# Two of four scaled token tiles take their places from another ring (L3 attention of a four-layer decoder)

## The chip, the core and the metric

The kernel is one program on one core of a Trainium2 chip. The core has five queues of instructions that run side by side: TensorE (PE, with its weight loads listed apart as PEld), VectorE (DVE), ScalarE (ACT), GpSimd (POOL) and SyncE (SP, which here only issues transfers). The metric is the device time of one execution in microseconds; lower is better. The time before is 3500.77 us, the median of three executions (3495.93 to 3503.63).

## The reference, cut to what matters

The reference runs four decoder layers over x of shape (8, 256, 256): 8 batches of 256 tokens with 256 features. Each layer is an attention, a cross attention and a feed-forward part, each added to x and normalised. The change lies in the attention of the last layer (L3), which is a state-space block rather than a softmax attention:

```
h = _rmsnorm(x, rms_w)
zxbcdt = h @ in_proj_w.T
...
conv = conv_b
for k in range(D_CONV):
    conv = conv + xp[:, k:k + l, :] * conv_w[:, k]
xBC = jax.nn.silu(conv)
...
dt = jax.nn.softplus(dt + dt_bias)
...
y = _ssd(xh, dt, A, B, C)
y = y + xh * Dp[None, None, :, None]
y = _rmsnorm(y * jax.nn.silu(z), norm_w)
out = y @ out_proj_w.T
return out + res
```

Only the first line concerns the change: every row of x is multiplied by its own 1/root-mean-square, and the scaled x must then lie transposed (features on partitions) for the product with in_proj_w. The weight rms_w is multiplied into in_proj_w elsewhere.

## The kernel before

**Tiles.** x lies in 16 tiles of 128 tokens x 256 features, X[0] to X[15]. Four tiles make a block of 512 tokens (blocks 0 to 3, called B0 to B3 below), and two tiles make a batch (batches 0 to 7). The L3 attention, `l3_attn`, works per block for what is cheap to do for 512 tokens at once, and per batch for the rest.

**A block.** `block(blk)` first waits for its X tiles (`need`), takes the reciprocal roots r of the mean squares on POOL (L183, L184, 128x4), and then, for t = 0 to 3, writes the scaled tile x = X * r (L2054 on ACT for block 0, L2056 on POOL for blocks 1 to 3), transposes it on PE (`transpose_to`, two instructions a tile at L302, eight a block), and copies the result from PSUM to the tile xr (`copy`, L142 on DVE and L144 on ACT in turn). `steps` then forms dt and its running sums for the block (L2071 to L2094).

**A batch.** `inputs` makes z, x, B and C (PE, L156), the convolution on DVE (L2148 and L2152) and two Silu passes on ACT. `weights` makes the decay matrices (PE L2176; DVE L2189 and ACT L2187; exp on ACT L2199; products on DVE L2206 and L2213). `outputs(b)`, called O0 to O7 below, makes y (PE L2227, DVE L2230, POOL L2235), its mean square (ACT L2239, PE L156, DVE L2245, POOL L183 and L184), and then, for each of the batch's two tiles: x2 = X + X on POOL (L2251), the output product on PE, r = product * r2 + x2 on DVE (L2255), and the layer norm of r (DVE L253, L255; POOL L183, L184; DVE L264), which is the new X tile.

**Rings.** The pool `tmp` keeps three places for each tag. A tile asked for under a tag takes one of its three places in turn, so it can be written only when the tile that held the place before has been read for the last time. Two tags matter here, both with places of 128x256 float32: "xb", which holds the four scaled tiles of a block and the x2 of `outputs`, and "res", which holds the r of `outputs` and, in the other layers, the r of `finish` (L280). Before the change, the xb places are asked for in this order: B0 t0 to t3, B1 t0 to t3, O0 x2 twice, B2 t0 to t3, O1 twice, O2 twice, B3 t0 to t3, O3 twice, and so on; the res places in the order O0 twice, O1 twice, O2 twice.

**Order.** The instructions are written in a Python program, with generators (`later`, `tick`, `fill`, `following`) that weave pieces of one batch between those of another. What is written is not yet the order of a queue: when the program is built, a planner goes through it with estimated durations, hands out the places of the rings, and fixes each engine's order; an instruction that is ready early by the plan can go ahead of one written earlier. In the trace, for one, x2 of batch 0 (L2251, 3013.12 us) runs ahead of the y product of the same batch (L2235, 3040.47 us), which is written before it. On the chip each engine then keeps its fixed order and waits at every instruction for what that needs.

Of the kernel before, what the change touches and what calls it, by code (L numbers as in the profile page):

```python
# [20 lines left out]
P = 128  # L21
NB = 8
S = 256
D = 256
# [37 lines left out]
class Build:  # L62
# [1916 lines left out]
    def l3_attn(self):  # L1979
        nc, a = self.nc, self.a  # L1980
        with ExitStack() as ctx:
# [62 lines left out]
            def block(blk):  # L2044

                self.need(2 * blk + 1)
                out = xrs[blk] = self.t(w2, [P, 2, 512], "xr")
                r = self.t(self.sm, [P, 4], "r4")
                self.rsqrt(r, self.ms[blk], 1.0, 1e-5)
                yield  # L2050
                for t in range(4):
                    x = self.t(self.tmp, [P, D], "xb")
                    if blk == 0:
                        nc.scalar.activation(x, self.X[4 * blk + t], AF.Copy, scale=r[:, t : t + 1])  # L2054
                    else:
                        nc.gpsimd.tensor_scalar(x, self.X[4 * blk + t], r[:, t : t + 1], 1.0, ALU.mult, ALU.mult)  # L2056
                    self.transpose_to(out[:, :, t * P : (t + 1) * P], x, 2)
                yield
                yield from steps(blk, out)

            def steps(blk, xr):
# [36 lines left out]
                sts[blk] = dt, cs, csT.rearrange("p i s -> p (i s)")  # L2098

            front = block(0)  # L2100
            fill(5)
            next(front)
# [167 lines left out]
            Es.append(self.t(w3, [P, 4, 384], "E", bufs=1))  # L2270
            xds = [free[:, 3072:].rearrange("p (t h d) -> p t h d", t=2, h=8), self.t(w3, [P, 2, 8, 64], "xd", bufs=1)]
            following = block(1)
            next(following)
            for b in range(NB):
                blk = b // 2
                if b % 2 == 0:
                    next(following, None)

                self.tick()
                E, xd = weights(b, cv, *sts[blk])  # L2280
                last = (b, cv, zs, E, xd)
                if b + 1 < NB:
                    cv, zs = inputs(b + 1, xrs[(b + 1) // 2])
                    if b % 2 == 0:
                        next(following, None)
                self.settle(1)
                if b % 2:
                    following = block(b // 2 + 2) if b // 2 + 2 < NBLK else iter(())
                    next(following, None)
                self.later(outputs(*last))  # L2290
# [672 lines left out]
```

## Time and profile before

| | |
|---|---|
| median of three executions | 3500.77 us (3495.93 to 3503.63) |
| the profiled execution | 3466.69 us, of which the span shown is 3465.0 us |
| TensorE clock granted, mean | 0.913 |
| the first scaled tile (L2054) | 2920.87 us after the span's start |
| the last scaled tile (L2056) | 3133.4 us |
| L2056 (POOL) | 12 times, 472 / 478 / 2693 ns (least, median, most) |
| L2054 (ACT) | 4 times, 493 / 502 / 510 ns |
| L2251 (POOL) | 16 times, 605 / 612 / 2055 ns |

The profile is of one execution, which was 34 us shorter than the median of the three timed ones. Times in it are counted from the start of its span. A row of the timeline gives start, duration, engine, line, operation, the tile written and the tiles read, shapes and count; in brackets stands how long the engine was idle before it and what ended that. Rows of a kind on one engine are merged, with a count. A row of the chain (the work that ended last, followed back) gives start, duration, engine, tile and line.

### The profile page before, as it was taken

The numbers are of one execution on the slowest core, as the hardware profiler recorded it, in microseconds if no ns is written. First come the engines' busy times: TensorE is split into PE (matmuls) and PEld (weight loads), VectorE is DVE, ScalarE is ACT, GpSimd is POOL, SyncE is SP. The second block draws the span as 40 slices with busy tenths as digits, with TensorE's granted clock in tenths as the row PEclk, the third lists the DMA queues.
The fourth block names the chain that finished last, engine by engine and source line by source line (L and its number), as shares of the span: only waits on it lengthen the run. The fifth ranks groups of instructions, "written<-read, shape, count | busy, mean of one in ns | idle before, by whom it ended". The sixth has DMA issues, their size and how long they took to land. (4 is left out here: it accounts for less than half of the span.)

```text
span 3465.0 us, 49405 instructions
## 1 busy us (share of the span) xinstructions
PE 3068.0 (89%) x19135; PEld 2169.0 (63%) x19146; DVE 1819.0 (52%) x4852; ACT 1055.4 (30%) x2386; POOL 911.1 (26%) x1370
## 2 busy tenths in 40 slices
PE   4777679989998998998999999898888998888789
PEld 3444357768886666665566776565555886676556
DVE  7887556641005656785111221576675344777652
ACT  4666422222222233332111111343222112344211
POOL 2222323343313211232000000322343454322241
PEclk6777779989999999999999999999777999988899
DMA  9900110025532000001010333100002562000000
GB/s 334 333 1 6 34 42 16 16 94 185 187 128 89 17 28 14 17 17 59 14 37 25 113 131 118 37 20 8 7 19 84 200 210 77 25 1 7 13 6 19
DMA packets 132672, 241.58 MB, mean 70 GB/s; under 512 B 14600, under 2 KB 103952, under 8 KB 124752
## 3 DMA queue, kind: packets, MB, share of 16 engines
q1 hardware_dynamic: 108176, 138.34, 11.8%
q0 software_dynamic: 23104, 98.95, 8.3%
q8 instruction: 155, 2.54, 0.3%
q10 hardware_dynamic: 1152, 1.05, 0.1%
q14 instruction: 85, 0.70, 0.1%
HBM read 158.61 MB, written 79.69 MB: 69 GB/s over the span
## 5 line engine op out<-in xcount | busy, mean ns | idle before, releaser
L156 PE MATMUL ps<-xt,w 128*128 128x256 f32 (+1 forms) x1408 | 444.6, 465 | 8.3 <-issue 8.3
L156 PE MATMUL ps<-w,hT 128*128 128x256 f32 (+1 forms) x1792 | 397.4, 380 | 0.0
L156 PEld LDWEIGHTS ps<-w,hT 128*128 128x128 f32 (+1 forms) x1792 | 330.5, 187 | 55.9 <-issue 6.0
L156 PE MATMUL ps<-gT,w 128*128 128x256 f32 (+1 forms) x1472 | 356.9, 401 | 5.7 <-ACT gT L144 3.0
L156 PEld LDWEIGHTS ps<-xt,w 128*128 128x128 f32 x1408 | 263.8, 194 | 150.5 <-issue 129.8
L156 PEld LDWEIGHTS ps<-gT,w 128*128 128x128 f32 x1472 | 276.8, 191 | 76.1 <-ACT gT L144 3.9
L156 PE MATMUL ps<-w,oT 128*128 128x256 f32 x768 | 184.1, 394 | 12.3 <-DVE oT L1423 11.2
L156 PEld LDWEIGHTS ps<-w,oT 128*128 128x128 f32 x768 | 147.7, 196 | 48.6 <-issue 12.6
L1147 ACT ACTIVATE hT<-ps,more 128x256 f32<-128x256 f32 x152 | 71.9, 473 | 199.1 <-PE ps L156 199.1
L236 PE MATMUL ps<-ident,x 128*128 128x128 f32 x320 | 64.8, 314 | 74.2 <-DVE x L264 57.3
L276 POOL TENSOR_TENSOR xb<-x,rows 128x256 f32<-128x256 f32 x96 | 74.0, 778 | 212.7 <-DVE res L281 205.5
L264 DVE TENSOR_SCALAR x<-res,mv,rs 128x256 f32<-128x256 f32 x128 | 58.8, 459 | 123.0 <-POOL rs L184 123.0
L1158 DVE COPY y<-ps 128x512 f32<-128x512 f32 x41 | 28.3, 690 | 174.6 <-PE ps L156 174.6
L1224 DVE TENSOR_TENSOR hT<-hT,ps 128x512 f32<-128x512 f32 x56 | 38.5, 687 | 150.6 <-PE ps L156 150.6
L686 ACT ACTIVATE e<-ps,nm 128x128 bf16<-128x128 f32 (+1 forms) x256 | 103.7, 459 | 40.1 <-DVE nm L681 24.1
L1220 ACT ACTIVATE hT<-ps 128x512 f32<-128x512 f32 x56 | 33.4, 597 | 238.5 <-PE ps L156 238.5
L1717 POOL TENSOR_TENSOR kpad<-kpad,rows 128x256 f32<-128x256 f32 (+1 forms) x10 | 7.3, 729 | 363.5 <-DVE hu L1666 276.2
L236 PEld LDWEIGHTS ps<-ident,x 128*128 128x128 f32 x320 | 39.5, 155 | 98.9 <-DVE x L264 44.9
L903 POOL TENSOR_TENSOR P<-P,z 128x1232 f32<-128x1232 f32 (+1 forms) x32 | 55.2, 1734 | 167.3 <-DVE z L902 167.3
L970 PE MATMUL ps<-PT,V 77*64 77x256 f32 x512 | 90.8, 413 | 6.9 <-ACT PT L144 4.4
L1581 ACT ACTIVATE f<-ps,neg 128x512 f32<-128x512 f32 x128 | 77.3, 688 | 57.7 <-PE ps L1578 57.7
L1582 DVE SCALAR_TENSOR_TENSOR f<-ps,f 128x512 f32<-128x512 f32 x128 | 79.1, 682 | 26.1 <-ACT f L1581 26.1
(665 smaller groups left out, 6344.7 us busy)
## 6 DMA issues: line engine op xcount, KB each, us to landing
l2x<-zero SPq DMA_DIRECT2D x28, 1024.0 KB, 11.4
l0x<-zero SPq DMA_DIRECT2D x16, 1024.0 KB, 11.4
w<-in_L_ffn_rg SPq DMA_DIRECT2D x8, 1024.0 KB, 7.1
w<-in_L_ffn_ru SPq DMA_DIRECT2D x8, 1024.0 KB, 5.0
w<-in_L_ffn_rd SPq DMA_DIRECT2D x8, 1024.0 KB, 5.4
l2e<-y SPq DMA_DIRECT2D x22, 256.0 KB, 2.3
rows<-in_rows SPq DMA_DIRECT2D x9, 544.0 KB, 3.7
l0e<-y SPq DMA_DIRECT2D x19, 256.0 KB, 2.7
```

The source lines that it names most:

```text
L156: self.nc.tensor.matmul(out, lhsT, rhs, start=(i == 0), stop=(i == last))
L236: self.nc.tensor.transpose(ps[:, k * P : (k + 1) * P], x[:, k * P : (k + 1) * P], self.ident)
L264: nc.vector.tensor_scalar(t, r, mv[:, 0:1], rs, ALU.subtract, ALU.mult)
L276: self.nc.gpsimd.tensor_tensor(t, self.X[i], row, ALU.add)
L686: nc.scalar.activation(e[:, : (t + 1) * P], ps[j][:, i, :], AF.Exp, bias=nm[:, t, h : h + 1], accum_out=z[:, t, h : h + 1],)
L903: eng.tensor_tensor(pr, pr, z.unsqueeze(2).to_broadcast([P, n, SC]), ALU.mult)
L970: nc.tensor.matmul(po[64 * m : 64 * m + 64, :S], V[:, h * 64 : (h + 1) * 64], ahead[n % 2][:, m, :], start=True, stop=True,)
L1147: nc.scalar.activation(hT[:, f + m, :], ps[:, m * 256 : (m + 1) * 256], func, bias=more[:, f + m : f + m + 1])
L1220: nc.scalar.activation(hT[:, f, :], ps, func, **({"bias": bias(f)} if bias else {}))
L1224: nc.vector.tensor_tensor(hT[:, f, :], hT[:, f, :], ps, ALU.mult)
L1581: nc.scalar.activation(f[:, j], ps[j], AF.Exp, bias=neg1)
L1582: self.mark = nc.vector.scalar_tensor_tensor(f[:, j], ps[j], 1.0, f[:, j], ALU.max, ALU.min)
```

## The change

The scaled tile is asked for under the tag "xb" for t = 0 and 1, as before, and under "res" for t = 2 and 3. Sizes, engines and arithmetic stay as they are, and so do the number of instructions and the memory taken. The order in which places are asked for becomes: on xb, B0 t0 t1, B1 t0 t1, O0 twice, B2 t0 t1, O1 twice, O2 twice, B3 t0 t1, O3 twice; on res, B0 t2 t3, B1 t2 t3, O0 twice, B2 t2 t3, O1 twice, O2 twice, B3 t2 t3, O3 twice.

```diff
                 for t in range(4):
-                    x = self.t(self.tmp, [P, D], "xb")
+                    x = self.t(self.tmp, [P, D], "xb" if t < 2 else "res")
                     if blk == 0:
                         nc.scalar.activation(x, self.X[4 * blk + t], AF.Copy, scale=r[:, t : t + 1])
```

## The prediction

> **What bounds the kernel now.** I read the page first, for the whole span.
>
> ```profile
> span 3465.0 us, 49405 instructions
> ...
> PE 3068.0 (89%) x19135; PEld 2169.0 (63%) x19146; DVE 1819.0 (52%) x4852; ACT 1055.4 (30%) x2386; POOL 911.1 (26%) x1370
> ```
>
> PE bounds the kernel as a whole, but the change sits in one late stage, so next come the stage's own windows: before, during and after the batches of L3 attention.
>
> ```profile
> 2870.00:3010.00 140.00, 118.53 (x461) 80.69 (x459) 76.63 (x238) 41.89 (x67) 61.79 (x102) 0.93 0.19 61
> 3010.00:3240.00 230.00, 194.21 (x1104) 160.38 (x1104) 174.59 (x444) 100.03 (x159) 53.00 (x83) 0.84 0.01 3
> 3240.00:3465.00 225.00, 184.45 (x744) 130.53 (x744) 90.92 (x264) 38.07 (x69) 62.12 (x116) 0.92 0.04 15
> ```
>
> (Columns: length, then busy PE, PEld, DVE, ACT, POOL, clock, DMA.) From 3010 to 3240 us PE is busy 84% and DVE 76%: they take turns, and neither is full. POOL, which writes 12 of the 16 scaled tiles, is busy 53 of 230 us. So a POOL wait costs only through who waits for POOL. The view of the writing line says that:
>
> ```profile
> L2056 POOL TENSOR_SCALAR xb<-x,r x12: 472/478/2693, 2943.3 to 3133.4; 128x256 f32<-128x256 f32 x12
> ...
>   DVE res L2255: 15.2, 3
>   DVE x L264: 9.5, 1
>   PE ps L302: 6.5, 2
> ...
>   PEld ps L302: 8.9, 3
>   PE ps L302: 8.3, 2
> ```
>
> The first three indented rows are what POOL waited for before writing: 15.2 us in 3 waits for the r of `outputs` (an xb place still held by an x2), 9.5 us once for a new X tile, 6.5 us in 2 waits for transposes (the place held by this block's own first tile). The last row is what it costs others: PE waited 8.3 us in 2 waits. Both are in the timeline:
>
> ```profile
> 3064.02 2.69 POOL L2056 TENSOR_SCALAR xb<-x,r 128x256 f32<-128x256 f32 x1 [4.79 <-PE ps L302]
> ...
> 3066.76 0.44 PE L302 MATMUL ps<-ident,xb 128*128 128x128 f32 x2 [2.42 <-POOL xb L2056]
> ...
> 3132.14 1.73 POOL L2056 TENSOR_SCALAR xb<-x,r 128x256 f32<-128x256 f32 x2 [9.45 <-DVE x L264]
> ...
> 3133.47 1.14 PE L302 MATMUL ps<-ident,xb 128*128 128x128 f32 x4 [5.88 <-POOL xb L2056]
> ```
>
> The first pair is the ring: B2's fourth tile waits for the transposes of its first, and PE then waits 2.42 us for it. The second pair is not: B3's third and fourth wait for X[14] and X[15] (DVE L264), which DVE wrote only at 3131.62 and 3132.34. Last I read the chain of what ended last, around the first pair:
>
> ```profile
> 3055.55 0.48 DVE res L2255
> 3056.04 0.66 DVE st L253 x2
> ...
> 3056.87 0.27 POOL rs L183
> ...
> 3058.40 0.20 POOL rs L183
> ...
> 3060.73 1.58 DVE w L2152 x4
> ...
> 3066.85 2.65 DVE w L2152 x4
> ...
> 3070.56 0.40 DVE w L2230
> ...
> 3071.01 1.52 PE ps L2227 x16
> ```
>
> The chain runs through DVE's convolution from 3059.3 to 3071, not through the late tile. PE's 2.42 us lie beside it: at 3071.01 PE waits again, for DVE L2230.
>
> **The change part by part.** It removes and adds no instruction; 16 scale instructions keep their 0.478 us (POOL) or 0.502 us (ACT), and no DMA and no SP work is touched. What moves is when a place is free, and with it the planned order.
>
> B0 (ACT, 2920.87 to 2931.45). Three tiles are written at 2920.87 to 2922.66, the fourth at 2930.94 behind B0's own transposes. With res free (its last earlier use, in routing, is at 2652 us) the fourth can follow the third. The chain there is ACT: two scaled tiles, hTs (L1907), the third tile, hTs, to 2923.15. If the fourth goes ahead of the last hTs, that is late by 0.50 us; if behind, ACT is idle 2.66 us soon after, and it costs nothing. PE's wait of 0.43 us at 2931.50 goes, but at that time the chain is in POOL's rsg and DVE's L264. I take 0, bounds -0.43 and +0.50.
>
> B1 (POOL). Three tiles run at 2943.33, the fourth at 3012.67. It now follows the third at about 2944.7, and O0's first x2 (0.61 us) can follow that; POOL is idle 7.44 us until 2952.17, and the gathers queue after it, so nothing is pushed. At 3012 the chain runs in PE without a gap: 5 transposes 1.17, 4 products 0.64, 3 transposes 0.74 us. Contiguous or not, they cost the same. I take 0; the bound below is -1.89 us, PE's wait just before (for POOL L2306, ended 3011.02), if the order let all transposes (1.17 + 0.74 = 1.91 us) fill it; above, 0.
>
> B2 (POOL). The first and second tile wait as before: t1 for O0's first r (3054.48). t2 no longer needs O0's second x2 place; t3 takes the place of O0's first r and waits for its norm (L264, 3057.80 + 0.41 = 3058.21) instead of B2's first transposes (3063.9). It is written some 5.5 us earlier. PE's 2.42 us go, covered by DVE, which is busy without a gap from 3059.3 to 3075; were that cover gone, up to -2.42. On the other side POOL's queue holds the two root pairs of O0's norm (3056.87 and 3058.40), which DVE's L264 waits for on the chain. O1's first x2 (0.61 us) becomes free at O0's second r (3056.03) and can slip in behind t2 (ends 3056.61): to 3057.22, that is 0.35 us past 3056.87. t3, ready at 3058.21, ends at 3058.69 against 3058.40: +0.29. Taken: +0.64. Bounds: -2.42 and +0.61 + 2.69 = +3.30 (the longest L2056 in the trace).
>
> One rule speaks here. The row: L2056 lasted 2.69 us at 3064.02, beside DVE's L2148 and L2152 back to back, against 0.478 in the median. The Trainium skill, "SBUF — State Buffer", section "Who interferes with whom", says that GpSimd and VectorE share one port pair, that an instruction which finds it held blocks until that one ends, and that a VectorE instruction with two SBUF inputs contends with a GpSimd one that reads. By that rule a moved tile waits for one L2152 (0.48), so t3 costs 0.96, and the sum of B2 would be about 0.35 + 0.77 = +1.1 us; by the row it is up to 2.5.
>
> B3 (POOL). t2 and t3 take places of O1 and O2 (r read by 3123.2), but X[14] and X[15] come at 3132 all the same. New waits on DVE: the r of O1 and O2 now need B2's transposes (about 3066) done; they are written at 3086.9 and 3118.5, so no wait. PE's 5.88 us stay: 0. Bounds: the nearest row is that wait itself, -5.88 if a new order puts O3's L2227, which stand behind it, first; +5.88 if such a wait arises once more.
>
> Later. O4 to O7 and the two parts after them ask for places as before. Their order can still change, since the planner's clock is shifted. Nearest row: PE's wait of 5.54 us for DVE L264 at 3244.51, so -5.54 to +5.54; taken 0.
>
> Sum: 0 + 0 + 0.64 + 0 + 0 = +0.6 us on the profiled 3466.69 us, 3467.3. On the median (34.08 us above the profiled execution) that is 3501.4; the terms know nothing below 1 us, and I say 3500. Ends: -0.43 - 1.89 - 2.42 - 5.88 - 5.54 = -16.2 and 0.50 + 3.30 + 5.88 + 5.54 = +15.2.
>
> **The rivals.**
>
> Same (the forecast): the orders stay nearly as they are, the removed waits were covered, and the tag of a place that wasn't what held B3 is no help. For it: the chain above. Time 3500, by itself 3494 to 3507.
>
> Faster: the earlier tiles let the planner order PE and DVE anew between 3010 and 3240. For it: PE and DVE are both idle at times there (36 and 55 us), and a fixed order that waits for one tile while 24 L2227 stand behind it (3133.47) is the kind of thing that a small shift undoes. Against: X[14] and X[15] don't depend on the rings changed. Price: 5.88 + 2.42 = 8.3 us, 3492.5; with B1's 1.89, 10.2 us, 3490.6. It decides against "same" from 7 us, that is, only if the 5.88 goes.
>
> Slower: the scaled tile and x2 that are free sooner go ahead of O0's root on POOL (+3.30 at most at B2), and the new order gives PE one more wait like that of 3133.47 at a place where the chain passes: +3.30 + 5.88 = 9.2 us, 3510. For it: four roots of two batches lie between these tiles, and POOL stretched L2056 to 2.69 us once. Against: it needs the second wait; the first alone is under 7 us. It decides when both fall on the chain.
>
> The change does nothing: if places are handed out in written order, B2's t3 waits as long as before by the plan, and all orders are equal. Time 3501, part of "same".
>
> **How the numbers follow.** 0.2% is 7 us, about what a measurement of this kernel tells from no change (the three runs span 7.7). "Same" gets 0.38, since no term that I take reaches 2 us. That the one planned order has to stand through 540 us is less sure than that: a shift of ready times reaches every queue from 2921 us on. So faster gets 0.36 and slower 0.26; faster is the larger, as every place is free no later than before, and only POOL's queue can lose. The range goes to both sums of ends, little widened for the runs' own spread: 3500.8 - 16.2 - 2 = 3482 and 3500.8 + 15.2 - 1 = 3515.
>
> **What would show it.** Right: L2056 has no wait for L302 any more; B1's four tiles stand in one row near 2943; PE's wait at B2's last transposes is gone; the chain between 3056 and 3071 still runs through L2152; the wait before B3's last transposes is still there, for L264. B2's step is wrong if POOL's roots of O0's norm come at the same time after the r as now. The prediction is wrong if the stretch from B2 to O7 gets shorter or longer by more than 7 us with other instructions in front of PE's waits, or if the difference lies after 3240 us, where nothing was changed.

## The result, and the profile after

The changed kernel takes 3499.55 us (median of 12 executions, 3491.84 to 3510.07) against 3499.94 us for the kernel before in the same comparison (12 executions, 3490.62 to 3506.93). The ratio is 1.0 with a 95% interval of 0.9987 to 1.0013: no difference that can be measured. The forecast was 3500.

The profiled execution after is 33.5 us longer than the one before, and that says nothing of the change. The page of after:

```profile
span 3498.5 us, 49398 instructions
...
PE 3086.9 (88%) x19135; PEld 2175.4 (62%) x19146; DVE 1817.6 (52%) x4852; ACT 1055.6 (30%) x2386; POOL 909.2 (26%) x1370
```

The 7 instructions fewer than before are semaphore instructions; the engines' counts are equal. The first scaled tile stands at 2953.32 us in it, against 2920.87: 32.45 of the 33.5 us are there before the first instruction that the change touches, where both programs have the same order of work. Nor does that part belong to the change: in a second profile of the changed kernel, shown below, the first scaled tile stands at 2924.48 us. So the change is read from the first scaled tile to the end: 544.10 us before, 545.17 after. The kernel before, profiled a second time, has 545.16, and the changed one 542.43.

The planned order hardly moved either. With the names of the places set aside, PE and SP issue the same sequence in both kernels (between 98 and 355 us, far ahead of the change, the records of some neighbouring matmuls stand in exchanged places). ACT has one instruction moved (B0's fourth tile, now ahead of the last hTs), DVE three (at about 2925 to 2937 us) and POOL eight.

What the change was to do, it did. The writing line in after, with what POOL waited for and who waited for it:

```profile
L2056 POOL TENSOR_SCALAR xb<-x,r x6: 472/479/482, 2977.0 to 3152.5; 128x256 f32<-128x256 f32 x6
L2056 POOL TENSOR_SCALAR res<-x,r x6: 472/477/1272, 2977.9 to 3167.5; 128x256 f32<-128x256 f32 x6
...
  DVE res L2255: 13.7, 2
  DVE x L264: 4.1, 1
...
  PE ps L302: 6.6, 1
```

The 6.5 us that POOL waited for transposes (L302) before a scaled tile are gone, and so is the tile of 2.69 us. PE's two waits for scaled tiles, 8.3 us, have become one of 6.6. The ring's wait itself has not gone from POOL, though: it is now the x2 of `outputs` that wait for transposes, 11.2 us in 3 waits, where before it was 0.5 us in one. No engine waits for an x2 in either kernel. The line of x2 in after:

```profile
L2251 POOL TENSOR_TENSOR xb<-x x16: 604/612/2055, 2978.8 to 3271.7; 128x256 f32<-128x256 f32 x16
...
  PE ps L302: 11.2, 3
```

POOL's timeline around B1 and B2 (start, duration, what it wrote, and in brackets the idle time before):

```profile
2976.97 0.94 POOL L2056 TENSOR_SCALAR xb<-x,r 128x256 f32<-128x256 f32 x2
2977.89 0.93 POOL L2056 TENSOR_SCALAR res<-x,r 128x256 f32<-128x256 f32 x2
...
3087.91 0.48 POOL L2056 TENSOR_SCALAR xb<-x,r 128x256 f32<-128x256 f32 x1 [6.01 <-DVE res L2255]
3089.56 0.61 POOL L2251 TENSOR_TENSOR xb<-x 128x256 f32<-128x256 f32 x1 [1.17 <-DVE res L2255]
...
3091.75 0.48 POOL L2056 TENSOR_SCALAR res<-x,r 128x256 f32<-128x256 f32 x1 [0.55 <-DVE mv L255]
...
3097.91 2.43 POOL L2251 TENSOR_TENSOR xb<-x 128x256 f32<-128x256 f32 x2 [4.76 <-PE ps L302]
```

B1's four tiles stand in one row. B2's fourth comes at 3091.75, 4.4 us after O0's first r (3087.33), where before it came 10.1 us after it (3064.02 against 3053.90). PE in the same stretch, and at B3:

```profile
3097.44 0.60 PE L302 MATMUL ps<-ident,xb 128*128 128x128 f32 x4
3097.88 0.60 PE L302 MATMUL ps<-ident,res 128*128 128x128 f32 x4
...
3104.43 0.87 PE L2227 MATMUL ps<-E,xd 128*64 128x256 f32 x8 [3.42 <-DVE w L2230]
...
3167.56 1.15 PE L302 MATMUL ps<-ident,res 128*128 128x128 f32 x4 [6.55 <-POOL res L2056]
```

The wait of 2.42 us at B2's last transposes is gone. The next one has grown in its place, from 1.28 us (3071.01, before) to 3.42, for the same DVE L2230: 3.70 us of waits became 3.42. At B3 PE waits for the same tile as before, 0.67 us longer (6.55 against 5.88 us). And the chain of work that ended last runs through DVE's convolution, as before:

```profile
3093.18 0.41 DVE x L264
...
3094.65 1.58 DVE w L2152 x4
...
3099.25 0.62 DVE w L2148
3099.87 1.15 DVE w L2152 x2
...
3101.34 1.58 DVE w L2152 x4
...
3103.98 0.40 DVE w L2230
...
3104.43 1.52 PE ps L2227 x16
```

Batch by batch, the two kernels lie on each other. The table gives the time from the first r (L2255) of one batch to that of the next, from the timelines, in us:

| | O0 | O1 | O2 | O3 | O4 | O5 | O6 | sum |
|---|---|---|---|---|---|---|---|---|
| before | 33.0 | 31.6 | 34.7 | 30.3 | 27.7 | 26.0 | 21.0 | 204.4 |
| before, second profile | 32.9 | 31.4 | 35.0 | 31.4 | 30.5 | 25.9 | 21.0 | 208.1 |
| after | 32.9 | 31.7 | 35.1 | 30.3 | 29.7 | 24.1 | 20.9 | 204.7 |
| after, second profile | 33.2 | 30.5 | 35.1 | 30.3 | 29.7 | 25.1 | 21.3 | 205.2 |

O4 differs by 2.8 us between two executions of the same kernel before. What differs there is the clock that TensorE was granted (0.94 in the first, 0.83 in the second). It is not steady in this stage: it switches between full and half speed. In before, after PE's wait of 2.42 + 1.28 us in O0 and one of 3.34 us in O1 (columns: stretch, length, busy PE, PEld, DVE, ACT, POOL, granted clock, DMA):

```profile
3076.00:3083.00 7.00, 7.00 (x26) 6.19 (x26) 1.91 (x4) 4.05 (x5) 0.91 (x2) 0.51 0.01 4
3083.00:3103.00 20.00, 15.51 (x105) 12.71 (x106) 19.28 (x59) 6.77 (x12) 2.72 (x7) 1.00 0.00 0
3103.00:3114.00 11.00, 10.83 (x51) 9.45 (x46) 4.98 (x13) 6.73 (x9) 3.40 (x4) 0.53 0.01 1
```

In after the same two drops come, as long as before and, within 0.2 us, at the same distance from the batch's r:

```profile
3109.70:3116.30 6.60, 6.60 (x23) 5.79 (x23) 1.84 (x4) 3.77 (x5) 0.91 (x2) 0.50 0.02 4
3116.50:3137.00 20.50, 16.07 (x111) 13.03 (x109) 19.78 (x60) 7.41 (x14) 2.72 (x7) 1.00 0.00 0
3137.00:3147.20 10.20, 9.92 (x42) 8.86 (x39) 4.34 (x12) 6.09 (x7) 3.40 (x4) 0.50 0.01 2
```

The last row reads: in 10.2 us at half speed, PE was busy 9.92 us for 42 matmuls; the row above it has 111 in 20.5 us, 16.07 busy.

### The profile page after: what moved, and what is told of

It is laid out like the page before. It is cut to its first block, busy times and chain, and to the rows that moved or that the text cites. A ratio compares the mean times of both kernels' runs of the same rounds, so it can differ in the third digit from the quotient of the medians.

```text
span 3498.5 us, 49398 instructions
## 1 busy us (share of the span) xinstructions
PE 3086.9 (88%) x19135; PEld 2175.4 (62%) x19146; DVE 1817.6 (52%) x4852; ACT 1055.6 (30%) x2386; POOL 909.2 (26%) x1370
## 3 DMA queue, kind: packets, MB, share of 16 engines
q8 instruction: 155, 2.54, 0.3%
## 5 line engine op out<-in xcount | busy, mean ns | idle before, releaser
L156 PE MATMUL ps<-w,oT 128*128 128x256 f32 x768 | 185.9, 397 | 12.2 <-DVE oT L1423 11.2
L1147 ACT ACTIVATE hT<-ps,more 128x256 f32<-128x256 f32 x152 | 71.6, 473 | 204.4 <-PE ps L156 195.4
L264 DVE TENSOR_SCALAR x<-res,mv,rs 128x256 f32<-128x256 f32 x128 | 58.8, 459 | 122.9 <-POOL rs L184 122.9
L970 PE MATMUL ps<-PT,V 77*64 77x256 f32 x512 | 92.6, 420 | 10.2 <-DVE PT L142 5.5
```

Of the source, the lines that this page charges most:

```text
L156: self.nc.tensor.matmul(out, lhsT, rhs, start=(i == 0), stop=(i == last))
L264: nc.vector.tensor_scalar(t, r, mv[:, 0:1], rs, ALU.subtract, ALU.mult)
L970: nc.tensor.matmul(po[64 * m : 64 * m + 64, :S], V[:, h * 64 : (h + 1) * 64], ahead[n % 2][:, m, :], start=True, stop=True,)
L1147: nc.scalar.activation(hT[:, f + m, :], ps[:, m * 256 : (m + 1) * 256], func, bias=more[:, f + m : f + m + 1])
```

## The experiments

The theory at this point: the change is carried out, but the wait it removes was covered by DVE, and the wait that counts (B3) isn't made by the ring. The rivals: the early tile is worth something and is paid back elsewhere (by ACT at B0, by POOL's roots); or the 5.88 us at B3 would have been the gain, and only that is missing. Medians of different sets of runs are up to 31 us apart for the same kernel (3499.94 and 3468.86), so every time stands beside the kernel before in its own set.

**How far two executions of one kernel differ.** The kernel before, without an edit.

> The kernel before, unchanged, profiled once more. The two profiles that there are differ by 33.5 us at the end, of which 32.4 us already at the first scaled tile, before which the two kernels have the same order on every engine. Theory A (the difference is one of executions): this profile's span comes near that of the changed kernel, 3490 to 3507 us, and from the first scaled tile to the end it takes 544.1 us as in the first profile of before, within 1 us. Theory B (the change costs something in the whole kernel): the span is again near 3465 us.

Measured: 3473.43 us, beside 3477.7 for the same kernel in the same set. From the first scaled tile to the end 545.16 us, 1.06 more than the first profile, with the batches of the table above. Neither expectation came as written: the span is 3471.7 us, nearer to 3465 than to 3490, and the stretch is 0.06 us outside the 1 us of theory A. What separates the two is the second profile of the changed kernel at the end of this section: its span of 3466.9 us is as short as those of the kernel before, so the long one belonged to the execution. Differences of 1 to 3 us in a batch can't be put down to the change from one profile.

**Each half alone.** Block 0 only, then blocks 1 to 3 only.

```diff
-                    x = self.t(self.tmp, [P, D], "xb")
+                    x = self.t(self.tmp, [P, D], "res" if blk == 0 and t > 1 else "xb")
```

> Only block 0's third and fourth tile (ACT) take places of res; blocks 1 to 3 are as before. Theory cover: the only cost of the change is ACT's fourth tile ahead of the last hTs, so against before the time from the first scaled tile to the end grows by 0.4 to 1.2 us, all of it by 25 us after the first tile. Theory offset (blocks 1 to 3 gain what block 0 loses): it grows by 3 us or more, since the gain of 2.4 us at block 2 is not there.

```diff
-                    x = self.t(self.tmp, [P, D], "xb")
+                    x = self.t(self.tmp, [P, D], "res" if blk > 0 and t > 1 else "xb")
```

> Only blocks 1 to 3 (POOL) take places of res; block 0 is as before. Theory cover: PE's wait of 2.42 us for block 2's fourth tile goes, PE's next wait for DVE L2230 grows from 1.28 to some 3.5 us, and the time from the first scaled tile to the end is that of before within 0.7 us. Theory offset: it shrinks by 2 us or more.

Measured: 3472.46 us (block 0) and 3471.69 us (blocks 1 to 3), beside 3473.43; from the first scaled tile to the end 543.58 and 543.70 against 545.16. Neither part costs or gains anything beyond what two executions differ by (1.06 us above, 2.74 for the changed kernel's two profiles). The growth of 0.4 to 1.2 us that was expected of block 0 alone can't be seen either: its stretch is 0.5 to 1.6 us shorter than those of the kernel before. The exchange of waits belongs to blocks 1 to 3: in the second profile of the kernel before, PE's timeline at B2 has two waits,

```profile
3070.03 0.44 PE L302 MATMUL ps<-ident,xb 128*128 128x128 f32 x2 [2.42 <-POOL xb L2056]
3074.27 0.87 PE L2227 MATMUL ps<-E,xd 128*64 128x256 f32 x8 [1.28 <-DVE w L2230]
```

and with blocks 1 to 3 changed, one:

```profile
3073.86 1.15 PE L2227 MATMUL ps<-E,xd 128*64 128x256 f32 x8 [3.42 <-DVE w L2230]
```

L2227 starts 17.1 us after O0's first r in both (r at 3057.15 and 3056.77), and so it does in the other profile of the kernel before and in the two of the changed one. The DVE work in front of it sets that time, wherever PE waits.

**The opposite: one place for all four tiles.** All scaled tiles are written to one tile that exists already, the kernel's tile of zeros, so each waits for the transposes of the one before.

```diff
-                    x = self.t(self.tmp, [P, D], "xb")
+                    x = self.zero
```

> The opposite dose: all four scaled tiles of a block take one single place, so that each waits for the transposes of the one before it, in all blocks. Theory cover: block 2's stall of PE grows from 2.4 us to three such turns, 5 to 9 us, of which the first 3.7 us (2.42 + 1.28) stay covered by DVE; with block 0 (three turns of ACT and PE, about 3 us), block 1 (three turns, about 4 us) and block 3 (one turn more, about 2 us) the time from the first scaled tile to the end grows by 3 to 14 us. Theory that ring waits never matter here: it grows by less than 2 us.

Measured: 3486.72 us beside 3473.43 and 3477.7, and 552.33 us from the first scaled tile to the end, 7.2 to 8.2 more than the kernel before. The writing line shows who waited:

```profile
  PE ps L302: 16.5, 9
...
  PE ps L302: 11.2, 7
```

(First row: POOL for transposes; second: PE for the tiles.) So the place of a scaled tile can cost time when all four share one. The size is not clean, though: the tile of zeros has other users, and a whole stretch of the order changed with it (SP's too), so the 7 to 8 us aren't the price of these waits alone.

**Take B3's wait away too.** The rival "faster" put 8.3 us on PE's two waits for scaled tiles. X[14] and X[15] are written earlier if all that is left of the part before (the feed-forward of L2, woven into this one) is asked for ahead of the batches (in the traces two DVE instructions, the L264 of these two tiles, leave O2 for the stretch ahead of O0): once with the rings of before, once with the changed ones.

```diff
-            inner.close()
+            self.need(NB - 1); inner.close()
```

> The kernel before, rings as before, with the last two X tiles (14 and 15) normalised before the batches of L3 attention start instead of after the convolution of batch 4. This takes away what block 3's third and fourth tile wait for, PE's 5.88 us. Theory cover (only that wait lies on the chain): PE's wait before block 3's last transposes falls below 1 us, and the time from the first scaled tile to the end falls from 544.1 to 545.2 us (two profiles of before) by 2 to 6 us; the ratio is 0.9983 to 0.9994. Theory that all waits for scaled tiles are covered: the wait goes, the time stays within 1.2 us.

> The same early normalisation together with the change of rings. Theory cover: like the kernel with early normalisation alone, within 1.2 us from the first scaled tile to the end. Rival (the rings pay once block 3's tiles are there early): 2 us or more better than with early normalisation alone.

Measured, with the old rings: 3497.9 us, ratio 1.0003 (0.9994 to 1.0013); with the changed rings 3498.33, ratio 1.0004 (0.9993 to 1.0015), both beside 3496.99. With the old rings only a part of PE's 8.3 us went. The wait for X is gone, and the ring, which now ends last, keeps POOL and PE waiting:

```profile
L2056 POOL TENSOR_SCALAR xb<-x,r x12: 472/478/3382, 2976.3 to 3158.6; 128x256 f32<-128x256 f32 x12
...
  PE ps L302: 11.3, 3
...
  PE ps L302: 5.5, 2
```

(First of the two rows: POOL for transposes; second: PE for the tiles.) PE's wait before B3's last transposes is 3.11 us, not under 1. From the first scaled tile to the end the profile has 541.19 us, 2.9 to 4.0 less than the kernel before, as the theory of the cover expected; the ratio that it expected (0.9983 to 0.9994) did not come. 3 us of the profile's gain lie in O1, where the clock was at half speed for 3.4 us instead of 10.2 and 6.8; O2 is shorter by 1.9 and 2.1 us.

With the changed rings no engine waits for a tile of L2056 at all. It isn't faster either, and its first profile, 551.50 us, fits neither expectation; the second has 541.87, within 1.2 us of the run with the old rings. By the interval, the gain is at most 0.07%, 2.4 us, where the rival said 8.3. Where the rest went is seen in O2, which held the 5.88 us. The kernel before, and then the kernel with early X and the changed rings (its second profile, introduced below):

```profile
3118.52:3153.26 34.74, 27.46 (x152) 21.74 (x151) 24.45 (x62) 14.05 (x24) 9.11 (x15) 0.80 0.05 17
```

```profile
3110.93:3145.02 34.09, 28.73 (x152) 24.10 (x151) 24.24 (x59) 14.17 (x24) 9.25 (x14) 0.75 0.05 17
...
3126.92 2.83 PE L2227 MATMUL ps<-l2s,xd 128*64 128x256 f32 x16 [3.39 <-DVE w L2230]
```

PE's idle time in O2 falls only from 7.28 us (34.74 - 27.46) to 5.36 (34.09 - 28.73), because a wait of 3.39 us for DVE L2230 comes up behind the one removed. And the same 152 matmuls take 1.27 us longer, at a lower granted clock (0.75 against 0.80). 1.92 - 1.27 = 0.65 us are left, which is the difference of the two lengths.

**The same kernel profiled twice more.** No edit; the changed kernel, and the one with early X and changed rings.

> The changed kernel, unchanged, for a second profiled execution. By both theories: L2056 without a wait for L302, PE's wait at B2's last transposes gone, the wait for L2230 behind it 3.4 us, first-to-end 543 to 547 us (545.2 in the first profile). By the clock-pattern theory the stretches between the batches' first r differ by up to 1 to 2 us one by one from those of the first profile (32.9, 31.7, 35.1, 30.3, 29.7, 24.1, 20.9).

> The kernel with earlier X tiles and the changed rings once more, unchanged, for a second profiled execution: no wait of PE for a scaled tile. The first profile had 551.5 us from the first scaled tile to the end at a mean granted clock of 0.861, the variant without the changed rings 541.2 at 0.890. Theory A (clock pattern, differing from execution to execution): first-to-end differs from 551.5 by more than 2 us, with the clock to match. Theory B (a fuller PE is always granted a lower clock): 550 to 553 at 0.86 again.

Measured: the changed kernel 3468.62 us (kernel before in this set: 3468.86), 542.43 us from the first scaled tile to the end where 543 to 547 were expected, with the waits as expected and the batches of the table above. The other one 3461.99 us, and 541.87 us from the first scaled tile to the end where its first profile had 551.50. Two thirds of these 9.6 us lie in one batch, O0. First profile and second:

```profile
3092.31:3128.77 36.46, 31.91 (x173) 27.55 (x172) 24.63 (x59) 13.52 (x23) 9.10 (x14) 0.81 0.00 1
```

```profile
3052.82:3082.78 29.96, 25.42 (x174) 21.81 (x173) 24.45 (x60) 13.52 (x23) 9.09 (x14) 1.00 0.00 1
```

The idle time of PE is 4.55 us in the one and 4.54 in the other, with the same two waits (1.0 and 3.42 us). PE's busy time is 6.49 us longer for the same matmuls: in the first profile the clock was at half speed for 13.7 us of the batch, in the second for none. That is 0.47 us per us at half speed, with nothing else changed. From O1 on the two profiles agree within 0.02 us a batch.

**Without the cover.** If DVE's convolution hides the late tile, a shorter convolution should uncover it. Two of the four taps are left out (12 of the 18 L2152 of a batch, so the output is another), once with the old rings and once with the new.

```diff
-                    for k in range(1, 4):
+                    for k in range(3, 4):
```

> The kernel before with two of the convolution's four taps left out (12 of 18 L2152 a batch, some 4.7 us of DVE a batch; the output is not the reference's). It takes away DVE's cover for block 2's fourth tile. PE's wait for that tile stays at 2 to 5 us, and PE no longer waits 1.28 us for L2230 after it. To be compared with the next run.

> The change of rings with the same two taps left out. Theory cover: now PE's wait for block 2's fourth tile is on the chain, so with the rings changed the stretch from O0's first r to O1's first r is shorter than in the run with the rings of before by 1.5 to 3 us. Theory that the wait is harmless for another reason (the rings give nothing even without cover): the same within 0.7 us.

Measured: 3466.14 us with the old rings and 3475.88 with the new, one execution each, where the kernel before took 3496.99; from the first scaled tile to the end 512.09 and 522.75 us. PE's waits for scaled tiles were 1.3 us in the one and 1.7 in the other, where 2 to 5 us had been expected for B2's tile alone: that wait was 0.21 us. So the uncovered tile wasn't there to be gained: with the shorter convolution the transposes come earlier as well, and the ring's wait shrinks by itself. From O0's first r to O1's it took 29.28 us with the old rings and 29.49 with the new, not 1.5 to 3 us less; PE's wait of 0.21 us was gone, and one for DVE L264 had grown from 0.78 to 1.35. This run therefore doesn't show what the tile would cost without its cover. The 10.7 us between the two point the wrong way, so both were run again, timed.

> The kernel before with two of the convolution's four taps left out (the first of its two L2152 products and sums is gone, so the output isn't the reference's). DVE, the cover of the late scaled tiles, is shorter by some 0.5 to 1 us an L2152 pair. One profile gave a stretch from the first scaled tile to the end of 512.1 us against 544 to 545 for the kernel before. Theory A (the 10.7 us between this kernel and its twin with the changed rings is the pattern of the granted clock in one execution): the timed median is 25 to 35 us under the kernel before, and this profile's first-to-end lies between 512 and 523, where it was 512.1. Theory B (the difference belongs to the rings): 512 +- 1.5 again, and timed 8 us or more below the twin.

> The same with the third and fourth scaled tile in the other ring. Theory A (clock pattern): timed within 5 us of the twin with the old rings, ratios to the kernel before equal within 0.15%; the profile's first-to-end moves by several us from the 522.75 seen before, with the mean granted clock of the stretch O0 to O7 (0.881 there, 0.932 in the twin) moving the other way. Theory B (rings cost time once the cover is short): timed 8 to 11 us above the twin, first-to-end 522.7 +- 1.5. Theory C (rings gain once the cover is short, the 1.3 us of PE waits for scaled tiles): 1 to 2 us below the twin, which would not be told from A.

Measured: old rings 3442.82 us, ratio to the kernel before 0.9921 (0.9907 to 0.9934); new rings 3446.52, ratio 0.9941 (0.9927 to 0.9955). The medians are 3.7 us apart and the intervals overlap, though four of the five executions with the new rings are longer than all five with the old, so a cost of a few us isn't excluded in this shortened kernel. From the first scaled tile to the end: 510.64 and 521.86. Neither theory holds as written. The two profiles of each kernel agree (512.09 and 510.64; 522.75 and 521.86), so the clock's pattern isn't drawn anew in each execution here; and the times are less far apart than the profiles. (In the two profiled executions the times differ by 2.6 us, because the one with the old rings reached its first scaled tile 8.6 us later, 2928.16 against 2919.58, in work that has the same order.) Most of the 11 us is time at half speed, though. O1 with the old rings:

```profile
3085.88:3110.65 24.77, 22.35 (x151) 18.51 (x150) 19.83 (x57) 13.28 (x20) 6.04 (x11) 1.00 0.00 1
...
3089.72 0.93 PE L236 MATMUL ps<-ident,x 128*128 128x128 f32 x4 [1.66 <-DVE pl L2080]
```

and with the new:

```profile
3078.17:3106.25 28.08, 25.54 (x150) 21.17 (x149) 19.84 (x56) 13.29 (x20) 6.04 (x11) 0.88 0.00 1
...
3082.01 0.93 PE L236 MATMUL ps<-ident,x 128*128 128x128 f32 x4 [1.79 <-DVE pl L2080]
```

In this batch the order of PE, DVE, ACT and POOL is the same in both and PE is idle 2.42 and 2.54 us, yet it is busy 3.19 us longer at a clock of 0.88 instead of 1.00. Over O0 to O7 the busy time of PE rises from 157.90 to 167.13 us, 9.2 of the 10.6 us by which that stage is longer. Why the clock drops twice in this batch with the new rings and never with the old isn't settled: the largest wait is 1.79 us in the one and 1.66 in the other, and DVE and POOL have a few instructions in another order only in the batches before and after it. Whether such a difference in PE's small gaps is enough, or the moment at which they come in the clock's pattern, no run separates.

## Why the prediction was right

**What bounds the stage: right.** PE and DVE take turns, the chain runs through L2152, and PE's 2.42 us lay beside it. The wait moved by one instruction group (2.42 + 1.28 became 3.42), PE's L2227 starts 17.1 us after O0's first r whether PE waited for the tile or not, and with either half of the change alone the time stayed.

**B0: its upper end came, not the value taken.** The fourth tile went ahead of the last hTs. The DVE instruction behind it (L2743) starts 2.70 us after the first scaled tile, against 2.30: +0.40 where 0 was taken and +0.50 was the bound. PE's 0.43 us at the last transposes went, as expected.

**B1: right.** Four tiles in one row, the x2 of O0 behind them, and POOL still idle for 6.19 us afterwards.

**B2: one part of the +0.64 came, and a part that the sum left out cancelled it.** "O1's first x2 slips behind t2: +0.35" cost nothing: t2 is written earlier still (3081.42, right after a root of O0 and 5.9 us ahead of O0's first r), the x2 alone stands ahead of the root (3089.56 to 3090.17), and POOL's first root starts 1.32 us after O0's second r in both kernels. "t3 between the two root pairs" did happen and cost more, one tile of 0.48 us instead of 0.29: the second X tile (L264) starts 4.19 us after that r instead of 3.71. This L264 is on the chain (3093.18 us, above). But from its start to the first L2230 it takes 10.80 us (3093.18 to 3103.98) against 11.30 before (3059.26 to 3070.56), so that L2230 starts 14.99 us after the r, against 15.01. The 0.50 us go with the x2 on POOL: where they run beside DVE's convolution, it is slower, in both profiles of both kernels. Before, three of them ran beside it, here in POOL's timeline and in the chain:

```profile
3066.68 2.15 POOL L2251 TENSOR_TENSOR xb<-x 128x256 f32<-128x256 f32 x3
```

```profile
3066.45 0.41 DVE w L2148
3066.85 2.65 DVE w L2152 x4
```

Elsewhere in the chain an L2148 takes 0.33 us and four L2152 take 1.58, so these are 0.08 + 1.07 = 1.15 us late. After, one x2 has gone ahead of the root and two are left beside the convolution (3097.91); there the L2148 at 3099.25 takes 0.62 and the two L2152 behind it 1.15 instead of 0.79, 0.29 + 0.36 = 0.65 us late. So the term should have been +0.48 - 0.50, about 0; that the two are equally large is luck, and the prediction had no term for the second. By its own sign (POOL's roots at the same time after the r) the step is half wrong: the first pair of roots is at the same time, the second is later.

The rule on the port shared by GpSimd and VectorE (the Trainium skill, "SBUF — State Buffer", "Who interferes with whom") would have made the term +1.1. Its price for t3 isn't tested: t3 took 0.48 us, but it ran beside a copy (DVE L142), not beside an L2152. The two x2 that did run beside L2148 and L2152 took 2.43 us instead of 1.22, so the two engines are slower beside each other there. The prediction's 2.5 us "by the row" leaves out its own +0.35; its terms give 0.35 + 0.29 + 2.21 = 2.85. The tile that no longer waits for the ring lost its 2.69 us.

**B3: right that the wait stays, but it grew.** POOL still waits for L264 (4.1 us); the change of ring can't touch that. PE's wait is 6.55 us in both profiles of the changed kernel and 5.88 in both of the kernel before, 0.67 us where 0 was taken. Again it is the x2: two of them, which before ran behind the scaled tiles (3133.84), now come ahead of these, held up by the ring until B3's first transposes are done:

```profile
3160.87 1.23 POOL L2251 TENSOR_TENSOR xb<-x 128x256 f32<-128x256 f32 x2 [4.76 <-PE ps L302]
```

DVE's L2148 and L2152 beside them take 0.73 and 0.83 us instead of 0.41 and 0.48, and the L264 that B3's third tile waits for starts 13.79 us after O2's first r instead of 13.11. In the length of O2 (35.1 us twice, against 34.7 and 35.0) it isn't clear of what two executions differ by.

**Later: the 0 was right, the fear behind its bounds was not.** The forecast feared that a shift of ready times reaches every queue. It left PE's order as it was. What moves the later batches is the granted clock, which the prediction read only as a column: its windows had 0.84 there, and no term was made of it.

**The rivals.** "Same" came. "The change does nothing" had the right time, but not what happened: t3 does come earlier, and twelve instructions moved on ACT, DVE and POOL. "Faster" had the right condition (only if the 5.88 us go) and the wrong price: with the 5.88 and the 2.42 us gone, the measured gain is at most 2.4 us, not 8.3. A wait on PE was priced at its length, though the wait behind it took most of it over, and in O2 the clock took some of the rest. "Slower" needed a second long wait, and none came. The chance of 0.36 for "faster" was too high for that reason.

## What to carry to other kernels

Before a wait is priced, look at the next wait of the same engine and at what releases that: if it is the other engine's chain and that ends later anyway, a longer wait there is all that the removal brings, as here with 2.42 + 1.28 and 3.42 us. A ring that is relieved can pass its wait to another user of its places, and so move that user's work beside something else. Where two engines take turns, the granted clock is a term of the sum of its own: compare busy time for the same instructions, not only idle time, before calling a stretch slower by waits. And profile the same kernel twice before reading a difference of less than 10 us out of two profiles.

## What the hardware showed beyond that

The clock of TensorE is at full or at half speed in this stage (1.00 or 0.5 in the rows above), and in the profiles here the stretches at half speed last 3.4, 6.8, 10.2, 13.7 or 17.1 us, multiples of 3.4. A us at half speed cost 0.47 us in the one pair of executions where PE's waits were equal. The Trainium skill, "TensorE: Matmul & The Clock Gate", "Part 1: The HAM clock gate", states a window of about 3.4 us and the two speeds, which these lengths bear out, and that the windows run freely, so the same kernel can meet them differently; O0 of one kernel in two executions, 36.46 and 29.96 us, fits that, though no run shows the windows themselves. Its section "HAM oscillation — how this bites in real kernels" warns of gaps over about 3.4 us. Here stretches at half speed followed gaps of 3.3 us, and in the shorter convolution with the new rings two came in a batch with no gap over 1.8 us, so that figure isn't a safe bound for this kernel.
